# A three-layer graph network on one Trainium2 core: two bias buffers, later norm loads, and a later store of the adjacency

## The chip, the cores and the metric

The kernel runs on one core of one Trainium2 chip. The metric is the device time of one execution in microseconds (us), and lower is better. Times are given as the median of several runs. Durations of single instructions come from one profiled execution, whose own time is given below.

## The reference

Two graph networks run one after the other on 1250 nodes with 1024 features and 20000 edges. The stage that matters here is the middle of the first network, in which three layers work on a node state `h` of 256 features. Cut to what matters:

```python
h = layernorm(x, ln_in_g, ln_in_b)
h = relu(h @ W1 + b1)
h = h @ W2 + b2
for i in range(3):
    agg = segment_sum(h[src], dst, num_segments=n)
    z = h + agg                                  # (A + 1) h, A = counts of edges
    z = relu(z @ layer_Wa[i] + layer_ba[i])
    z = z @ layer_Wb[i] + layer_bb[i]            # layer_bb: the "second bias"
    z = relu(layernorm(z, layer_ng[i], layer_nb[i]))   # ng, nb: the "norm vectors"
    h = h + z
delta = relu(h @ Wd1 + bd1) @ Wd2 + bd2
return layernorm(x + delta, out_g, out_b)
```

The second network takes the mean over the neighbours with the same edges in two larger layers of 1024 features (about two thirds of the kernel's time). It uses the same adjacency matrix, without the diagonal, scaled by 1/degree.

## The kernel before

**Number format.** Every float32 operand of a matrix product is held as a high part and a low part (`split_w`, lines 133 to 135: ScalarE copies the high part at L134, VectorE takes the rest at L135), and each product is three matmuls (`mm3`, lines 122 to 125).

**Adjacency.** The 1250x1254 count matrix `A` is built in SBUF from one-hot matmuls, with the diagonal added. It serves the three layers of the first network. For the second network it is stored to memory, `A_d`, in one transfer of 6270 KB (L799), because its room in SBUF (pool tag "A") is then taken by `AD`, which holds the hidden values of the decoder (L811, written at L162 to L165 by `hidden`). It is loaded again, tile by tile, at L1165.

**One layer** (lines 769 to 808). `agg` (L667) is the product of `h` and `A` in three column chunks of 384, 512 and 358 and two halves of the features; it leaves `zh` (L672, ScalarE) and `zl` (L673, VectorE). `z1_chunk` is the product with `Wa`, bias and relu (L160 to L165). `z2_rows` takes ten row tiles: the product with `Wb`, one more matmul that adds the second bias from `bbc` (L697), the statistics, the scaling by the norm vectors `ngc` (L701) and `nbc` (L702), the sum with `h` (L704), and the split of the new `h` (L705 on ScalarE, L706 on GpSimd). The aggregation of the next layer (`agg(i + 1, ...)`) is mixed with the last rows of the present one, so that TensorE has work while rows are normalised.

**Loads of a layer.** `begin_layer(i)` (L643 to L653) loads the bias `bb[i]` as one row of 1 KB (L647), splits it with `split_w` into row 0 of `bbc` and a scratch row (L648), sends the scratch row to row 1 of `bbc` by a transfer in SBUF (L649), and loads the norm vectors, each repeated to 128 partitions (128 KB, L650 and L651). There is one `bbc`, one `ngc` and one `nbc`, so a layer's values can only be written when the last row of the layer before has been read. Layer i+1 is begun in the text behind the last rows of layer i (L793). Behind it, in the text, come for i = 0 the store of `A` (L799), the weights of layer 2 (`load_wab(2)`, L633), the decoder's bias (`load_bdo`: four loads of 256 KB at L737, then VectorE L738, L740, L743 and ScalarE L739, L742, L744) and three quarters of the decoder's second weight (`load_Wd2`, six loads at L725); for i = 1 the decoder's first weight (`load_Wd1`, L716) and the last quarter (L725).

**A ring of three.** All these raw loads, the two scratch rows of `begin_layer` among them, go through one ring of three buffers, `wraw` (L130), in the order of the text. A buffer is free again when its last reader is done.

**What sets the order.** In this stage the order on each engine is not written by hand (the hand-written parts are in `manual_schedule` blocks before and behind it). A planner lays out the program ahead of time with its own estimates of durations: on each engine it takes, among the instructions that are ready by its estimate, the one that stands first in the text. What comes out is fixed, and each engine, and SP's queue of transfers, then runs its list in that order: an instruction that has to wait holds up all that stands behind it. `tc.issue_after(x)` makes the planner place a transfer behind `x` on the same engine. All loads and stores named here are issued by SP; GpSimd issues the ones of `xo_d` (L754, L755) and `vt` (L926).

Beside the layers, `load_xo` writes x plus a bias row to memory: SP's L750 writes 5120 KB and GpSimd's L754 adds x to it in memory, 5 transfers.

Of the kernel before, what the change touches and what calls it, by code (L numbers as in the profile page):

```python
# [10 lines left out]
F32 = mybir.dt.float32  # L11
F32R = mybir.dt.float32r
# [3 lines left out]
AF = mybir.ActivationFunctionType  # L16
# [5 lines left out]
P = 128  # L22
N = 1250
NG = 4
NN = N + NG
# [3 lines left out]
DB = 256  # L29
# [26 lines left out]
def gz(t):  # L56
    return P if t < NT - 1 else N - (NT - 1) * P + NG
# [17 lines left out]
def gnn(ctx, tc, fli, general, x, es, vecs, W1, W2, b2, Wa, Wb, bb, ng, nb, Wd1, Wd2, bd2, og, ob,  # L75
        Ws0, Wn0, b0l, Ws1, Wn1, b1l, out):
    nc = tc.nc
    V, S, G, T = nc.vector, nc.scalar, nc.gpsimd, nc.tensor
# [7 lines left out]
    A_d = dram.tile([P, NT, NN], F32, name="A_d")  # L86
# [6 lines left out]
    def bcast(ap, n):  # L93
        return bass.AP(tensor=ap.tensor, offset=ap.offset, ap=[[0, P], [1, n]])
# [5 lines left out]
    ones = const.tile([P, P], F32, name="ones")  # L100
# [4 lines left out]
    def stats_to_rstd(mv, n):  # L105

        sd = small.tile([P, 1], F32, name="sd")
        S.activation(sd[:n], mv[:n, 1:2], AF.Sqrt, bias=epsc[:n])
        rs = small.tile([P, 1], F32, name="rs")
        V.reciprocal(rs[:n], sd[:n])  # L110
        return rs

    def bnstats(src, n, width):
        k = (width + 511) // 512
        st = small.tile([P, 2, 6], F32, name="st")
        for i in range(k):
            V.bn_stats(st[:n, i, :], src[:n, i * 512:min(width, i * 512 + 512)])
        mv = small.tile([P, 2], F32, name="mv")
        V.bn_aggr(mv[:n], st[:n, :k, :])
        return mv  # L120

    def mm3(ps, a_hi, a_lo, b_hi, b_lo, start, stop, go_on=False):
        T.matmul(ps, a_hi, b_hi, start=start, stop=False, skip_group_check=go_on)  # L123
        T.matmul(ps, a_hi, b_lo, start=False, stop=False, skip_group_check=go_on)  # L124
        T.matmul(ps, a_lo, b_hi, start=False, stop=stop, skip_group_check=go_on)  # L125

    def pst(name, tag="ps", dt=F32):
        return psp.tile([P, 512], dt, name=name, tag=tag)

    def wraw():  # L130
        return ring.tile([P, 512], F32, name="wraw")

    def split_w(raw, hi, lo, eng=V):
        S.activation(hi, raw, AF.Copy)  # L134
        return eng.tensor_sub(lo, raw, hi.bitcast(F32))  # L135
# [262 lines left out]
    def any_edges():  # L398

        acc = Ap.tile([P, NT, AW], F32, name="acc", tag="A")  # L400
        V.memset(acc, 0.0)
        scratch = [B1.tile([P, 8 * (PW + 2)], F32, name=f"g{s}", tag=f"h0{s}0", bufs=1) for s in "hl"] + spare
        general_adjacency(tc, psp, acc[:, :, :N], (esrc, est[:, ne:2 * ne]), ident, ones, x, A_g, xg_d, scratch)
        res = Ap.tile([P, NT, AW], F32R, name="A", tag="A")
        nc.sync.dma_start(res.bitcast(F32)[:, :, :NN], A_g)
        return res
# [6 lines left out]
    def new_h(i):  # L413
        return [[hpool.tile([P, 5, DB], F32R, name=f"h{i}{s}{j}", tag=f"h{s}{j}", bufs=2) for j in range(2)]
                for s in "hl"]
# [157 lines left out]
    for c in range(NC):  # L573
        if c == 1:
            A = any_edges() if general else Ap.tile([P, NT, AW], F32R, name="A", tag="A")
# [32 lines left out]
    B2 = tc.alloc_tile_pool(name="B2", bufs=1, side="right", reuse_waits="tile")  # L608
# [17 lines left out]
    L = {}  # L626
    loads = {}
# [8 lines left out]
        L[i] = dict(ps={}, w=(wh, wl))  # L636


    bbc = B2.tile([P, DB], F32R, name="bbc")
    S.activation(bbc[:, :P], ones, AF.Copy, scale=0.0)  # L640
    S.activation(bbc[:, P:], ones, AF.Copy, scale=0.0)

    def begin_layer(i):  # L643
        ngc, nbc = (B2.tile([P, DB], F32, name=nm_, tag=nm_, bufs=1) for nm_ in ("ngc", "nbc"))
        bbr = wraw()[0:1, :DB]
        bbl = wraw()[0:1, :DB]
        nc.sync.dma_start(bbr, bass.AP(tensor=bb.tensor, offset=bb.offset + i * DB, ap=[[DB, 1], [1, DB]]))  # L647
        split_w(bbr, bbc[0:1], bbl)  # L648
        nc.sync.dma_start(bbc[1:2].bitcast(F32), bbl)  # L649
        nc.sync.dma_start(ngc, bcast(ng[i], DB))  # L650
        loads["nb"] = nc.sync.dma_start(nbc, bcast(nb[i], DB))  # L651
        z = new_z(("zh", "zl")) + new_z(("z1h", "z1l")) if i else z_first + new_z(("z1h", "z1l"))
        L[i].update(vecs=(bbc, ngc, nbc), z=z)  # L653

    def new_z(names):
        return [[B2.tile([P, NN], F32R, name=f"{nm_}{k}", tag=f"{nm_}{k}") for k in range(2)] for nm_ in names]

    def agg(i, c, t0, t1, fs=(0, 1)):
        c0, w = CL[c]
        for f in fs:  # L660
            if t0 == 0:
                L[i]["ps"][c, f] = pst("ps_z", "pa")
            ps = L[i]["ps"][c, f]
            for t in range(t0, t1):
                n = gz(t)
                for s, hx in enumerate((hh, hl)):
                    T.matmul(ps[:, :w], hx[t // 5][:n, t % 5, f * P:(f + 1) * P], A[:n, t, c0:c0 + w],  # L667
                             start=(t == 0 and s == 0), stop=(t == NT - 1 and s == 1))
            if t1 == NT:
                zh, zl = L[i]["z"][:2]  # L670
                cs = slice(c0, c0 + w)
                S.activation(zh[f][:, cs], ps[:, :w], AF.Copy)  # L672
                V.tensor_sub(zl[f][:, cs], ps[:, :w], zh[f][:, cs].bitcast(F32))  # L673
# [14 lines left out]
    def z2_rows(i, t, nh, nl):  # L688
        n = gz(t)
        ts_ = slice(t * P, t * P + n)  # L690
        z1h, z1l = L[i]["z"][2:]
        wh, wl = L[i]["w"]
        bbc, ngc, nbc = L[i]["vecs"]
        ps = pst("ps_z2")
        for k in range(2):
            mm3(ps[:n, :DB], z1h[k][:, ts_], z1l[k][:, ts_], wh[:, 2 + k], wl[:, 2 + k], k == 0, False)
        T.matmul(ps[:n, :DB], onesr[:, :n], bbc, start=False, stop=True)  # L697
        z2 = B2.tile([P, DB], F32, name="z2", tag="z2", bufs=2)
        mv = bnstats(ps, n, DB)
        rs = stats_to_rstd(mv, n)  # L700
        V.scalar_tensor_tensor(z2[:n], ps[:n, :DB], mv[:n, 0:1], ngc[:n], ALU.subtract, ALU.mult)  # L701
        V.scalar_tensor_tensor(z2[:n], z2[:n], rs[:n], nbc[:n], ALU.mult, ALU.add)  # L702
        h = hf[t // 5][:n, t % 5]
        V.scalar_tensor_tensor(h, z2[:n], 0.0, h, ALU.max, ALU.add)  # L704
        S.activation(nh[t // 5][:n, t % 5], h, AF.Copy)  # L705
        G.tensor_sub(nl[t // 5][:n, t % 5], h, nh[t // 5][:n, t % 5].bitcast(F32))  # L706
# [39 lines left out]
    def load_xo():  # L746

        o = C3.tile([P, D], F32, name="o", tag="wt")
        nc.sync.dma_start(o, bcast(ob, D))
        nc.sync.dma_start(xo_d.rearrange("t p f -> p t f"), o.unsqueeze(1).broadcast_to([P, NT, D]))  # L750
        rows = xo_d.rearrange("t p f -> (t p) f")
        for t in range(0, NT, 2):
            r0, r1 = t * P, min(N, t * P + 2 * P)
            G.dma_start(rows[r0:r1], x[r0:r1], accum_op=ALU.add, max_dma_last_dim=8 * D)  # L754
        G.dma_start(rows[N:NN], xg_d, accum_op=ALU.add, max_dma_last_dim=4 * D)  # L755

    z_first = new_z(("zh", "zl"))
    load_wab(1)
    load_wab(0)
    begin_layer(0)  # L760
    load_xo()
    for t in range(EARLY + 1, NT):
        for half, cs in zip(sums, HALVES):
# [5 lines left out]
    for i in range(3):  # L769
        nh, nl = new_h(i)  # L770

        def rows(*ts):
            for t in ts:
                z2_rows(i, t, nh, nl)

        z1_chunk(i, 0)
        z1_chunk(i, 1)
        rows(0, 1)
        agg(i, 2, 0, 5, (0,))
        rows(2, 3)  # L780
        agg(i, 2, 5, NT, (0,))
        if i == 1:
            degrees()
        rows(4)
        agg(i, 2, 0, NT, (1,))
        rows(5, 6)
        if i == 2:
            break
        z1_chunk(i, 2)
        hh, hl = nh, nl  # L790
        agg(i + 1, 0, 0, 4)
        rows(7, 8, 9)
        begin_layer(i + 1)  # L793
        agg(i + 1, 1, 0, 4)
        agg(i + 1, 0, 4, 7)
        agg(i + 1, 1, 4, 7)
        if i == 0:
            with tc.issue_after(loads["nb"].ins):
                nc.sync.dma_start(A_d, A.bitcast(F32)[:, :, :NN])  # L799
            load_wab(2)  # L800
            load_bdo()
            for k in range(3):
                load_Wd2(k)
        else:
            load_Wd1()
            load_Wd2(3)
        agg(i + 1, 0, 7, NT)
        agg(i + 1, 1, 7, NT)


    AD = Ap.tile([P, NT, AW], F32R, name="AD", tag="A")  # L811
# [349 lines left out]
    A, loaded = {}, []  # L1161
# [523 lines left out]
```

## Time and profile before

| | us |
|---|---|
| median of 3 runs (lowest, highest) | 915.53 (914.59, 917.31) |
| time of the profiled execution | 917.94 |
| its span, first to last instruction | 916.1 |
| TensorE busy in the span | 891.3 (97%) |
| VectorE busy | 649.6 (71%) |
| ScalarE busy | 393.0 (43%) |
| GpSimd busy | 79.2 (9%) |
| mean granted clock of TensorE | 0.990 |

The profiled execution took 1.84 us more than its span and 2.41 us more than the median of the runs. TensorE is busy for nearly the whole span, so a change can only win where TensorE waits, and it loses wherever it makes TensorE wait. The three layers lie from 121 to 248 us. Busy time of TensorE is a union of overlapping matmuls: one of 256 columns is shown with 0.28 us, but the next one starts 0.12 us later. Where a matter of a few us is at stake, the starts of the matmuls say more than the busy share.

### The profile page before, as it was taken

Reading aid. Unit: us, or ns where it says so; the run is one execution under the profiler, and the core shown is the slowest. Engines: PE = TensorE matmul, PEld = TensorE weight load, DVE = VectorE, ACT = ScalarE, POOL = GpSimd, SP = SyncE. Lnnn points to the kernel's source line nnn. Section 1 sums busy time; section 2 is a strip of 40 time slices with the busy share of each in tenths; the row PEclk is TensorE's granted clock in tenths of the full one; section 3 lists DMA queues with packets and bytes.
Section 4 is the critical chain, followed back from the end, with each engine's and each line's share of the span. In section 5 each row is a group of like instructions: output and inputs, shape, how many; then the busy total and the mean of one; then the engine's idle time right before and its main releaser. Section 6 shows DMA issues by size and latency. Waiting matters only on the chain.

```text
span 916.1 us, 13254 instructions
## 1 busy us (share of the span) xinstructions
PE 891.3 (97%) x4783; PEld 783.0 (85%) x4783; DVE 649.6 (71%) x1335; ACT 393.0 (43%) x760; POOL 79.2 (9%) x106
## 2 busy tenths in 40 slices
PE   7899999999999999999999999999999999999995
PEld 5799999888987778999988888889999888888884
DVE  7999778597976776565586775447566776776883
ACT  3776524455467872111234355443112233333552
POOL 2223345121301000000000000000000000000000
PEclk8999999999999999999999999999999999999998
DMA  8310069953207569896622246538885722222223
GB/s 255 106 42 2 1 254 204 335 151 104 70 24 253 185 241 333 311 301 230 222 72 81 81 141 204 180 121 304 289 276 197 230 70 81 78 80 74 69 95 133
DMA packets 83668, 148.40 MB, mean 162 GB/s; under 512 B 8296, under 2 KB 31995, under 8 KB 83082
## 3 DMA queue, kind: packets, MB, share of 16 engines
q1 hardware_dynamic: 77206, 126.92, 41.4%
q0 software_dynamic: 2176, 10.27, 4.4%
q10 hardware_dynamic: 4212, 10.27, 3.0%
q8 instruction: 39, 0.64, 0.3%
q14 instruction: 35, 0.29, 0.1%
HBM read 103.37 MB, written 49.21 MB: 167 GB/s over the span
## 4 chain that ended last, share of the span: by engine, by line
PE 84%; DVE 8%; issue 3%; ACT 2%; DMA 1%; POOL 0%; POOLq 0%; ACTq 0%; DVEq 0%
PE ps_A L1237 20%; PE ps_m L123 14%; PE ps_m L125 14%; PE ps_m L124 14%; PE ps_z L667 4%; PE ps_dd L123 2%; PE ps_dd L125 2%; PE ps_dd L124 2%; PE pa L367 1%; PE ps_y L123 1%; PE pt L989 1%; PE pt L1258 1%; PE ps_y L124 1%; PE ps_y L125 1%; PE ps_z L124 1%
## 5 line engine op out<-in xcount | busy, mean ns | idle before, releaser
L123 PE MATMUL ps_m<-w,th 128*128 128x512 f32 x520 | 204.0, 392 | 0.0
L125 PE MATMUL ps_m<-w,th 128*128 128x512 f32 x520 | 202.5, 389 | 0.0
L124 PE MATMUL ps_m<-w,th 128*128 128x512 f32 x520 | 202.3, 389 | 0.0
L1237 PE MATMUL ps_A<-A,qh 128*128 128x418 f32 (+1 forms) x480 | 170.8, 356 | 0.0
L1237 PE MATMUL ps_A<-A,ql 128*128 128x418 f32 (+1 forms) x480 | 169.3, 353 | 0.0
L125 PEld LDWEIGHTS ps_m<-w,th 128*128 128x128 f32 x520 | 97.6, 188 | 20.6
L124 PEld LDWEIGHTS ps_m<-w,th 128*128 128x128 f32 x520 | 97.7, 188 | 19.9
L123 PEld LDWEIGHTS ps_m<-w,th 128*128 128x128 f32 x520 | 97.7, 188 | 19.6
L135 DVE TENSOR_TENSOR w<-stage,w 128x512 fp32r<-128x512 f32 x65 | 44.7, 690 | 68.1 <-ACT w L134 67.7
L1237 PEld LDWEIGHTS ps_A<-A,qh 128*128 128x128 f32 (+1 forms) x480 | 90.3, 188 | 2.0 <-DVE c L1220 0.4
L1237 PEld LDWEIGHTS ps_A<-A,ql 128*128 128x128 f32 (+1 forms) x480 | 90.7, 189 | 1.4
L134 ACT ACTIVATE w<-stage 128x512 fp32r<-128x512 f32 x65 | 40.7, 629 | 118.9 <-PE ps_m L125 78.9
L1242 DVE TENSOR_TENSOR MT<-ps_A,dgb 128x418 f32<-128x418 f32 x48 | 25.5, 586 | 64.4 <-PE ps_A L1237 64.4
L1198 ACT ACTIVATE qh<-qraw 128x1280 fp32r<-128x1280 f32 (+3 forms) x28 | 21.5, 808 | 104.3 <-PE ps_A L1237 87.0
L123 PE MATMUL ps_y<-h0h,w1h 128*128 128x256 f32 (+2 forms) x160 | 53.3, 333 | 0.4 <-ACT h0h L455 0.4
L135 DVE TENSOR_TENSOR w<-wraw,w 128x512 fp32r<-128x512 f32 x39 | 26.9, 689 | 32.7 <-ACT w L134 32.6
L1326 DVE TENSOR_TENSOR c<-ps_m,c 128x512 f32<-128x512 f32 (+1 forms) x65 | 40.9, 682 | 8.8 <-PE ps_m L125 8.7
L124 PE MATMUL ps_y<-h0l,w1h 128*128 128x256 f32 (+2 forms) x160 | 45.8, 286 | 1.0 <-DVE h0l L457 0.9
L125 PE MATMUL ps_y<-h0h,w1l 128*128 128x256 f32 (+2 forms) x160 | 45.5, 284 | 0.0
L1067 ACT ACTIVATE th<-XT 128x640 fp32r<-128x640 f32 x48 | 34.2, 725 | 20.5 <-DVE MT L1242 20.5
L134 ACT ACTIVATE w<-wraw 128x512 fp32r<-128x512 f32 x39 | 24.5, 628 | 41.9 <-PE ps_m L125 21.3
L1068 DVE TENSOR_TENSOR th<-XT,th 128x640 fp32r<-128x640 f32 x48 | 39.5, 822 | 0.0
(311 smaller groups left out, 1829.7 us busy)
## 6 DMA issues: line engine op xcount, KB each, us to landing
A<-A_d SPq DMA_DIRECT2D x20, 627.0 KB
w_d<-stage SPq DMA_DIRECT2D x43, 256.0 KB
stage<-w_d SPq DMA_DIRECT2D x43, 256.0 KB
stage<-in_l_W_neigh_dram SPq DMA_DIRECT2D x42, 256.0 KB
stage<-in_l_W_self_dram SPq DMA_DIRECT2D x28, 256.0 KB
A_d<-A SPq DMA_DIRECT2D x1, 6270.0 KB
wraw<-in_l_W_neigh_dram SPq DMA_DIRECT2D x22, 256.0 KB
w_d<-wraw SPq DMA_DIRECT2D x21, 256.0 KB
```

Of the source, the lines that this page charges most:

```text
L123: T.matmul(ps, a_hi, b_hi, start=start, stop=False, skip_group_check=go_on)
L124: T.matmul(ps, a_hi, b_lo, start=False, stop=False, skip_group_check=go_on)
L125: T.matmul(ps, a_lo, b_hi, start=False, stop=stop, skip_group_check=go_on)
L134: S.activation(hi, raw, AF.Copy)
L135: return eng.tensor_sub(lo, raw, hi.bitcast(F32))
L667: T.matmul(ps[:, :w], hx[t // 5][:n, t % 5, f * P:(f + 1) * P], A[:n, t, c0:c0 + w], start=(t == 0 and s == 0), stop=(t == NT - 1 and s == 1))
L1067: S.activation(hi, src, AF.Copy)
L1068: V.tensor_sub(lo, src, hi.bitcast(F32))
L1198: S.activation(q[0][:, t0:t1], raw[:, t0:t1], AF.Copy)
L1237: T.matmul(pss[j][c][:, :w], qs[j][s][:n, t], A_of(t)[:n, c0:c0 + w], start=start and s == 0, stop=stop and s == 1)
L1242: V.tensor_mul(MT[:, f, c0:c0 + w], pss[j][c][:, :w], dgb[:, c0:c0 + w])
L1326: V.tensor_add(c, ps[:n], c if last or M in (6, 7) else c11[:n, t])
```

## The change

The bias buffer `bbc` is made twice, and layer i uses number i mod 2. The two loads of the norm vectors move out of `begin_layer` into a function `load_norm`, which is called at the end of the loop's body, behind the other loads; for layer 0 it is called directly behind `begin_layer(0)`. The store of `A` moves from the loop's pass i = 0, where it stood behind layer 1's norm loads and ahead of `load_wab(2)`, to pass i = 1, behind layer 2's norm loads.

```diff
-    bbc = B2.tile([P, DB], F32R, name="bbc")
-    S.activation(bbc[:, :P], ones, AF.Copy, scale=0.0)
-    S.activation(bbc[:, P:], ones, AF.Copy, scale=0.0)
+    bbcs = [B2.tile([P, DB], F32R, name=f"bbc{i}") for i in range(2)]
+    for bbc in bbcs:
+        S.activation(bbc[:, :P], ones, AF.Copy, scale=0.0)
+        S.activation(bbc[:, P:], ones, AF.Copy, scale=0.0)
 
     def begin_layer(i):
-        ngc, nbc = (B2.tile([P, DB], F32, name=nm_, tag=nm_, bufs=1) for nm_ in ("ngc", "nbc"))
+        bbc = bbcs[i % 2]
         bbr = wraw()[0:1, :DB]
         bbl = wraw()[0:1, :DB]
         nc.sync.dma_start(bbr, bass.AP(tensor=bb.tensor, offset=bb.offset + i * DB, ap=[[DB, 1], [1, DB]]))
         split_w(bbr, bbc[0:1], bbl)
         nc.sync.dma_start(bbc[1:2].bitcast(F32), bbl)
+        z = new_z(("zh", "zl")) + new_z(("z1h", "z1l")) if i else z_first + new_z(("z1h", "z1l"))
+        L[i].update(bbc=bbc, z=z)
+
+    def load_norm(i):
+        ngc, nbc = L[i]["norm"] = [B2.tile([P, DB], F32, name=nm_, tag=nm_, bufs=1) for nm_ in ("ngc", "nbc")]
         nc.sync.dma_start(ngc, bcast(ng[i], DB))
         loads["nb"] = nc.sync.dma_start(nbc, bcast(nb[i], DB))
-        z = new_z(("zh", "zl")) + new_z(("z1h", "z1l")) if i else z_first + new_z(("z1h", "z1l"))
-        L[i].update(vecs=(bbc, ngc, nbc), z=z)
...
-        bbc, ngc, nbc = L[i]["vecs"]
+        bbc, (ngc, nbc) = L[i]["bbc"], L[i]["norm"]
...
     begin_layer(0)
+    load_norm(0)
     load_xo()
...
         if i == 0:
-            with tc.issue_after(loads["nb"].ins):
-                nc.sync.dma_start(A_d, A.bitcast(F32)[:, :, :NN])
             load_wab(2)
             load_bdo()
             for k in range(3):
...
             load_Wd2(3)
         agg(i + 1, 0, 7, NT)
         agg(i + 1, 1, 7, NT)
+        load_norm(i + 1)
+        if i == 1:
+            with tc.issue_after(loads["nb"].ins):
+                nc.sync.dma_start(A_d, A.bitcast(F32)[:, :, :NN])
```

## The prediction, made before the changed kernel was run

> **What bounds the kernel now.** I began with the busy shares and the chain of work that ended last: TensorE, busy 97% and 84% of the chain. So a gain must come from places where TensorE stands, and the next view is who it waited for during the layers (176 to 222 us, layer 1's pass). The columns are the total wait, the times, and the longest.
>
> ```profile
> PE ps_z L124 <- DVE zl L673: 1.2, 1, 1.2
> PE ps_z L125 <- DVE z1l L165: 0.8, 1, 0.8
> PE ps_z L123 <- ACT z1h L162: 0.4, 1, 0.4
> PE ps_z L667 <- POOL h1l L706: 0.2, 1, 0.2
> ```
>
> The same view for layer 0's pass (138 to 176 us) is empty. Overlapping matmuls hide part of the loss, so I measure it by starts. The first 512-column z1 matmul starts at 139.53 in layer 0, 177.54 in layer 1 and 222.31 in layer 2. Layer 0 takes 38.01 us, layer 1 44.77 us, with the same matmuls and the six of the degrees (L619), which displace 2.1 us (186.95 to about 189.06). **Layer 1 loses 44.77 - 38.01 - 2.1 = 4.66 us.** That is what there is to win. Four places, each measured against the usual distance of starts, make 4.3 of it: 1.9 in the last z1 chunk (its twelve matmuls span 3.68 us, 1.80 in layer 0), 0.55 before 202.97, 0.9 before 208.44, 0.9 in the aggregation at 215 to 217.4.
>
> Why do they occur? The timeline of SP's queue (start, duration, line):
>
> ```profile
> 128.81 0.64 SPq L649 DMA_DIRECT2D bbc<-wraw  x1
> 129.55 1.18 SPq L647 DMA_DIRECT2D wraw<-in_layer_bb_dram  x1
> 139.36 0.38 SPq L633 DMA_DIRECT2D wraw<-in_layer_Wa_dram  x1
> 164.09 0.54 SPq L649 DMA_DIRECT2D bbc<-wraw  x1
> 164.72 0.54 SPq L633 DMA_DIRECT2D wraw<-in_layer_Wb_dram  x1
> ...
> 166.43 0.64 SPq L799 DMA_DIRECT2D A_d<-A  x1
> 168.95 2.22 SPq L737 DMA_DIRECT2D wraw<-in_bd_dram  x1
> 171.28 1.68 SPq L737 DMA_DIRECT2D wraw<-in_out_b_dram  x1
> 173.51 0.92 SPq L737 DMA_DIRECT2D wraw<-in_bd_dram  x1
> 192.22 0.33 SPq L737 DMA_DIRECT2D wraw<-in_out_b_dram  x1
> ```
>
> and its waits:
>
> ```profile
> SPq L649 <- DVE wraw L135: 27.9, 3, 24.3
> SPq L737 <- DMA wraw<-in_out_b_dram: 16.5, 1, 16.5
> SPq L633 <- DMA bbc<-wraw: 8.6, 1, 8.6
> ```
>
> Layer 1's bias sits in the ring from 129.55 and stops SP for 24.3 us, since its split has to wait for layer 0's last row (162.1). Then the store of 6270 KB goes out ahead of the decoder's bias loads, and the first of ob's lands only at 173.51 + 0.92 + 16.5 = 190.9. So the fourteen pieces of work on bdo and the six splits of Wd2 fall on 191 to 211, among layer 1's rows:
>
> ```profile
> 195.51 0.69 DVE L738 TENSOR_TENSOR wraw<-wraw 128x512 f32<-128x512 f32 x1 [1.31 <-DMA wraw<-in_out_b_dram]
> 196.23 0.69 DVE L743 TENSOR_TENSOR wraw<-wraw,bdo 64x512 f32<-64x512 f32 x1
> 196.95 0.16 DVE L110 RECIPROCAL rs<-sd 128x1 f32<-128x1 f32 x1
> 197.03 0.51 DVE L673 TENSOR_TENSOR zl<-ps_z,zh 128x358 fp32r<-128x358 f32 x1
> ```
>
> TensorE's longest wait (1.2 us) is for that zl, which stands in line behind a subtraction that waits for ob. The wait at 202.97 is ScalarE's L742, L134 and L744 ahead of z1h, the one at 208.44 VectorE's Wd2 splits ahead of z1l, and the one at 216 is row 9: its bias matmul comes 22.3 us after the layer's mark in layer 0 and 31.6 in layer 1.
>
> **The change, part by part.**
>
> Second `bbc`: two more fills on ScalarE, 2 x 0.29 us at about 120.9. The list behind them waits 2.62 us for a load at 125.86, and the split of tile 9 at 121.78 is needed by matmuls at 134.5, so they cost nothing; without that cover 0.6.
>
> Layer 1's bias no longer waits for row 9. Its two ring buffers come free about 20 us earlier; Wb of layer 2 and the first bd load take them. Wa and Wb themselves still wait for layer 0's last row (one tile with the weights of layer 0), so the next buffers come free at the splits, 167.3 in the trace.
>
> The store leaves the queue there: the loads behind it get the engines. A load of 256 KB without it took 2.7 us at 201.55 (landed by 204.23). Work to place: on VectorE 6 x 0.69 for bdo and 6 x 0.69 for Wd2, 8.3 us; on ScalarE 8 x 0.63 and 6 x 0.63, 8.8 us. Room between 160 and 180: VectorE is idle for 9.0 us there (busy 4.42, 1.98, 1.93 and 2.65 in the four windows of 5 us), ScalarE for 11.7. From 180 to 190 VectorE is busy 9.4 of 10. Since the loads come three at a time from about 165, the bias part and some splits fit ahead of the rows and a few splits don't. I take back 0.5 us for those (lowest 0, highest the whole 4.3).
>
> The norm loads move behind others. They are freed by row 9 (L702 ends at 165.7) and needed at 183.2; if a ring load stands ahead of them they wait a few us of these 17. In layer 2 they are freed at 214.3 and needed at 229.0. Nothing; once 17 us are used up, each us costs one.
>
> Layer 2: Wd2's last quarter (VectorE L135 at 223.89, ahead of z1l) comes before the boundary. TensorE loses 0.25 us at 225.97 to it; gain 0.25.
>
> The store in its new place: freed by nbc of layer 2, so at 214.3 + 0.9 less what layer 1 has gained by then (3.4), about 211.8. Its own time is bounded by 17.0 us (6.42 MB at the 377 GB/s mean of 170 to 185 us) and 24.5 us (166.43 to 190.9). It lands between 229 and 236. DMA there is 0.0 to 0.56 busy. The new waiter is `AD`, which takes A's room: its first write is ScalarE's L162 at 244.44, 240.4 after the gain. Margin 4 to 11 us: nothing. Behind it on SP stand weights used at 284 and `ogc`, issued at 248. GpSimd's `vt` loads run on another queue and are needed from 252.6.
>
> Sum: 4.3 + 0.25 - 0.5 = **4.0 us less**. The profiled execution, 917.94, would become 913.9; it stands 2.41 above the median, so from 915.53 I forecast **911.5**. TensorE waits for nothing over 0.2 us from 330 on, so the gain should last to the end.
>
> **A rule against the row.** Layer 0's bias row of 1 KB, issued at 128.81 behind the 5120 KB store of L750, lands when SP's wait ends, 139.36: 10.5 us. Layer 1's bias load stands right behind it. Its split could now be listed early, ahead of ScalarE's first zh (135.04). The Trainium skill, DMA: Bandwidth & Descriptors, section Latency and other measured facts, puts the fixed cost of a transfer at some 2 us; by that, an estimate, the row would be there at 132 and this would cost nothing. The measured 10.5 us decides.
>
> **Rivals.**
>
> *Half a gain.* Either the planner puts the bias split ahead of zh: zh slips to 139.4 + 0.4, its first pair ends at about 140.3 and z1, which starts at 137.43, loses 2.9 (3.9 with zl behind it): 4.0 - 3.4, 914.9. Or the bdo and Wd2 work lands on the busy 181 to 200 and gives back half: 913.5. For it: instructions standing ready first in the text go first. Against it: the planner put L738 behind four rows of layer 1, close to when ob landed, so it does know of big transfers. Middle 914.2.
>
> *Slower: the decoder waits for the store.* If the weight loads of L1036 (220.97 to 224.94 now, each waiting for a ring buffer) are listed ahead of the norm loads, the store goes out at 225 and lands at 242 to 249.5, and AD's first write, with ScalarE's list behind it and soon all four banks of TensorE, waits up to 9.1 us. It decides from an issue at 215.9 (slow store) or 223.4 (fast). Price at the slow end 9.1 - 4.0: up to 920.6; I name 919. Against it: the norm loads come first in the text and are ready before most ring buffers.
>
> *More.* All 4.66 goes, and the work moved off VectorE also frees the wait for hT at 241.54 (0.76) and the two of 0.4 behind it: 909.3.
>
> **Chances.** Forecast (910 to 913) 0.56, half a gain 0.22, slower 0.14, more 0.08. A measurement can tell about 0.3%, 2.75 us, from no change. Faster by over that (under 912.8): 0.53 + 0.08 = 0.61. Within it: 0.03 + 0.21 = 0.24. Slower: 0.01 + 0.14 = 0.15. Range: 908.5 to 917.0, which leaves out most of the slower case and the edge of the best.
>
> **What would show it.** Right: layer 1 from mark to mark at about 40.5 us, no 24.3 us wait of L649, the first ob load landed by about 172, TensorE's waits for zl, z1h and z1l gone, the store issued at about 212 and no wait of AD's writers for it. Wrong: ScalarE or VectorE waiting for the bias row at 131 to 140; L701 waiting for ngc; L162 waiting for the store; Wd2 splits still ahead of z1l at 203 to 208.

## The result, and the profile after

The changed kernel takes 918.97 us (median of 14 runs, 916.66 to 920.51), the kernel before, run beside it, 917.24 (14 runs, 914.59 to 919.38). The ratio of the runs is **1.0027, 95% interval 1.0017 to 1.0037: about 2.5 us slower** (the two medians are 1.7 us apart). The forecast was 911.5, the range ended at 917.0, and the sign was wrong. The profiled execution took 919.0 us with a span of 917.2 (before: 917.94 and 916.1).

I measure it as the prediction did, from the start of the first 512-column z1 matmul of one layer to that of the next, and from layer 2's to the decoder's first matmul (`ps_dd`). The marks lie at 138.33, 179.97, 224.57 and 249.20 us, before at 139.53, 177.54, 222.31 and 247.83:

| us | before | after | difference |
|---|---|---|---|
| layer 0 (to layer 1's mark) | 38.01 | 41.64 | +3.63 |
| layer 1 (to layer 2's mark) | 44.77 | 44.60 | -0.17 |
| layer 2 (to the decoder) | 25.52 | 24.63 | -0.89 |
| sum | 108.30 | 110.87 | +2.57 |

The sum agrees with the ratio. (The two profiled executions differ by 1.1 us only, mainly because the one of before reaches its first mark 1.20 us later.) Layer 1, from which 4 us were to come, gave almost nothing, and layer 0, which had no loss at all, lost 3.6. Here is who TensorE waits for from 174 to 222 us (total, times, longest), to be read beside the four lines of before at the head of the prediction:

```profile
PE ps_z L123 <- ACT zh L676: 2.0, 2, 1.8
PE ps_d L619 <- DVE z L705: 1.5, 2, 1.2
PE ps_z L124 <- DVE zl L677: 1.1, 3, 0.4
PE ps_z L125 <- DVE z1l L165: 0.2, 1, 0.2
```

The waits have moved. TensorE now stands at the head of layer 1 for zh and zl, the evacuations of the aggregation, and then at the degrees (L619), whose PSUM bank is freed late by a row's L705. The timeline of SP's queue shows the change doing what it says:

```profile
144.54 0.54 SPq L650 DMA_DIRECT2D bbc<-wraw  x1
145.17 0.54 SPq L633 DMA_DIRECT2D wraw<-in_layer_Wb_dram  x1
150.22 0.35 SPq L741 DMA_DIRECT2D wraw<-in_bd_dram  x1
163.97 0.35 SPq L741 DMA_DIRECT2D wraw<-in_out_b_dram  x1
165.26 0.33 SPq L656 DMA_DIRECT2D ngc<-in_layer_ng_dram  x1
...
171.81 0.33 SPq L741 DMA_DIRECT2D wraw<-in_out_b_dram  x1
175.94 9.21 SPq L729 DMA_DIRECT2D wraw<-in_Wd_dram  x6
```

Layer 1's bias is through at 144.54 instead of 164.09, and no store stands ahead of the decoder's bias loads. `bdo`, the decoder's bias, holds bd2 - ob in three bf16 parts. Each half of 512 columns needs one load of bd2 and one of ob, and then a chain of seven pieces of work in turn, three subtractions on VectorE and four copies on ScalarE. The first load of ob, which needs the third buffer of the ring, waits until 163.97, when the split of Wa gives that buffer back. On VectorE (first line) and ScalarE (the others) the work that waits for it then looks like this:

```profile
171.08 0.69 DVE L742 TENSOR_TENSOR wraw<-wraw 128x512 f32<-128x512 f32 x1 [4.18 <-DMA wraw<-in_out_b_dram]
```

```profile
171.81 0.63 ACT L743 ACTIVATE bdo<-wraw 128x512 bf16<-128x512 f32 x1 [4.46 <-DVE wraw L742]
173.20 1.27 ACT L746 ACTIVATE bdo<-wraw 32x512 bf16<-32x512 f32 x2 [0.76 <-DVE wraw L744]
175.22 0.63 ACT L748 ACTIVATE bdo<-wraw 64x512 bf16<-64x512 f32 x1 [0.76 <-DVE wraw L747]
175.95 0.63 ACT L743 ACTIVATE bdo<-wraw 128x512 bf16<-128x512 f32 x1
176.48 0.85 ACT L676 ACTIVATE zh<-ps_z 128x384 fp32r<-128x384 f32 x2
```

Both engines stand over 4 us for ob, 7.1 us under way (163.97 to 171.08). Then the chain of the first half goes to and fro between them, each step waiting for the other engine, and takes 4.8 us for 2.1 us of work on VectorE and 2.5 on ScalarE. Layer 1's first zh stands behind it in ScalarE's list and comes at 176.48. In the kernel before, it waited for its matmul alone, and the chain stood behind layer 1's row 3:

```profile
171.79 0.49 ACT L672 ACTIVATE zh<-ps_z 128x384 fp32r<-128x384 f32 x1 [0.71 <-PE ps_z L667]
```

### The profile page after: what moved, and what is told of

It reads as the page before. It is cut to its first block, busy times and chain, and to the rows that moved or that the text cites. A ratio compares the mean times of both kernels' runs of the same rounds, so it can differ in the third digit from the quotient of the medians.

```text
span 917.2 us, 13254 instructions
## 1 busy us (share of the span) xinstructions
PE 892.2 (97%) x4783; PEld 783.2 (85%) x4783; DVE 649.2 (71%) x1335; ACT 393.1 (43%) x762; POOL 77.8 (8%) x106
## 4 chain that ended last, share of the span: by engine, by line
PE 83%; DVE 9%; issue 3%; ACT 2%; DMA 2%; POOL 0%; POOLq 0%; SPq 0%; DVEq 0%; ACTq 0%
PE ps_A L1244 20%; PE ps_m L123 14%; PE ps_m L125 14%; PE ps_m L124 14%; PE ps_z L671 4%; PE ps_dd L123 2%; PE ps_dd L125 2%; PE ps_dd L124 2%; DVE hf L708 1%; PE pa L367 1%; PE ps_y L123 1%; PE pt L996 1%; PE pt L1265 1%; DVE z L706 1%; PE ps_y L124 1%
```

## The theories, and experiments on which part it is

**Theory A**: the loss is this chain, listed ahead of layer 1's zh and zl and waiting there for ob. **Theory B**: it is the store in its new place, by its traffic after 215 us. **Theory C**: it is the norm vectors' new place. Four kernels do parts of the change.

### Two bias buffers alone

```diff
-    bbc = B2.tile([P, DB], F32R, name="bbc")
+    bbcs = [B2.tile([P, DB], F32R, name=f"bbc{i}") for i in range(2)]
...
+        bbc = bbcs[i % 2]
```

> The kernel before with the two bias buffers alone: norm vectors and store stay where they were. Theory A (the loss is the chain that makes bdo: it is now listed on ScalarE and VectorE ahead of layer 1's own zh and zl, and stands there for ob's load, 7 us under way): in this kernel's order the first half of the chain stands ahead of zh of 128x384 and the second half with the Wd2 splits behind row 3, as before, so layer 0 (first 512-column z1 matmul of layer 0 to that of layer 1) should be 40 to 42 us against 38.0 before and 41.6 in the changed kernel, layer 1 about 44.8, and the time 2 to 4 us above before. Theory B (the store's new place costs it, by its traffic after 215 us): the store hasn't moved, so the time is that of before, within 1 us. Theory C (the norm loads' new place): the same as B.

Measured: 919.97 us, ratio to before 1.0040 (1.0023 to 1.0056); layer 0 41.32 us, layer 1 46.90, layer 2 24.64. Layer 0 and the time are those of theory A. Layer 1 lost 2.1 us more than I had expected: the second half of the chain runs at 195 to 201 us there, among the rows, as it did before, while the first half has already cost its time in layer 0.

### The store one layer later alone

```diff
-            with tc.issue_after(loads["nb"].ins):
-                nc.sync.dma_start(A_d, A.bitcast(F32)[:, :, :NN])
...
         agg(i + 1, 1, 7, NT)
+        if i == 1:
+            with tc.issue_after(loads["nb"].ins):
+                nc.sync.dma_start(A_d, A.bitcast(F32)[:, :, :NN])
```

> The kernel before with the store alone one layer later; one bias buffer, norm loads as before. Theory A: without the store ahead of them the loads of bd2 and ob land at about 174 us instead of 190, and the order puts the chain of bdo among the four zh and zl of layer 1, so layer 0 is 40 to 43 us and the time 1 to 4 us above before. Theory B: slower by the whole 2.5 us, but with layer 0 at 38.0 and the loss behind 215 us. Theory C: as before, within 1 us.

Measured: 918.59 us, ratio 1.0022 (1.0010 to 1.0034); layer 0 41.47, layer 1 42.75, layer 2 26.47. The loss is in layer 0, where the store is not, so theory B falls. (Layer 2, where the store now runs, is 0.95 us longer here, but 0.89 shorter in the changed kernel.) With one buffer only, this kernel makes the same loss: freeing the queue is enough to pull the chain forward.

### The changed kernel with the store put back

```diff
-        if i == 1:
+        if i == 0:
             with tc.issue_after(loads["nb"].ins):
```

> The changed kernel with the store put back into the pass of layer 0, behind the norm vectors of layer 1. Theory A: the first half of bdo's chain is still listed ahead of zh, its ob is issued ahead of the store and lands at about 171 us, so layer 0 is 40 to 42 us; the second half and Wd2 stand behind row 3 again and layer 1 is about 44.8; the time is 2 to 4 us above before, so no better than the changed kernel. Theory B: the time goes back to that of before, or below it by what the early bias brings (0 to 4 us faster than the changed kernel). Theory C: no nearer to before than the changed kernel, with layer 0 unlike theory A at 38 to 39.

Measured: 920.04 us, ratio 1.0039 (1.0024 to 1.0055); layer 0 43.37, layer 1 43.69, layer 2 24.64. No nearer to before than the changed kernel, as theory A has it. Layer 0 was longer than expected, layer 1 shorter.

### The norm vectors later alone

```diff
         agg(i + 1, 1, 7, NT)
+        load_norm(i + 1)
+        if i == 0:
+            with tc.issue_after(loads["nb"].ins):
+                nc.sync.dma_start(A_d, A.bitcast(F32)[:, :, :NN])
```

> The kernel before with the loads of the norm vectors alone put behind the layer's other loads (the store behind them, as they are what it waits for). Theory A: the order keeps bdo's chain behind row 3, so layer 0 stays at 38.0, layer 1 at about 44.8, and the time within 1 us of before. Theory B: within 1 us of before. Theory C: 1.5 to 3 us slower than before.

Measured: 916.98 us, ratio 1.0004 (0.9994 to 1.0014); 38.01, 44.75, 25.62. No effect, and here the chain stands behind row 3. Theory C falls. (The store waits for the norm vectors and so moves in the text with them; it went out at 168.21, behind one load of bd2 and ahead of both loads of ob.) In all four kernels the time goes with the place of the chain.

## Is it the wait or the work?

**Theory A1**: what costs is that the chain stands ahead of zh and waits there for a late load. **Theory A2**: what costs is its work and that of the Wd2 splits, on two engines that have no room for it anywhere near.

### The chain held behind zl

```diff
-            V.tensor_sub(d, d, o)
-            S.activation(bdo[:, fs], d, AF.Copy)
+            with tc.issue_after(loads["zl"].ins):
+                V.tensor_sub(d, d, o)
+                S.activation(bdo[:, fs], d, AF.Copy)
...
         load_norm(i + 1)
+        if i == 0:
+            load_bdo()
+            for k in range(3):
+                load_Wd2(k)
```

(`loads["zl"]` is the last L677 of the aggregation; the calls stood ahead of its last tiles.)

> The changed kernel with bdo and Wd2(0..2) written behind layer 1's whole aggregation, and the first two steps of each half of bdo's chain held on ScalarE and VectorE until the last zl of that aggregation is issued; the loads are issued in the same order as in the changed kernel. Theory A1 (what costs is that the chain stands, waiting for ob, ahead of zh and zl): layer 0 goes back from 41.6 to 38.0 to 39 us, layer 1 stays at 44.6 to 46, and the time is 1.5 to 4 us below the changed kernel. Theory A2 (what costs is the chain's and the splits' work itself on two engines that have no room at the head of a layer, wherever it stands): layer 0 38 to 39, but layer 1 grows by as much, 47 to 48, and the time is that of the changed kernel within 1 us.

Measured: 915.11 us, ratio to before 0.9986 (0.9975 to 0.9997), against 1.0027 for the changed kernel: 3.8 us below it. Layer 0 38.84, layer 1 43.34, layer 2 24.51. Same loads, same work, another place in two lists: 2.8 us of layer 0 are back and layer 1 didn't grow. This is theory A1. VectorE's first step of the chain comes behind the last zl and waits for nothing, and the first zh comes at 171.16:

```profile
176.24 0.68 DVE L743 TENSOR_TENSOR wraw<-wraw 128x512 f32<-128x512 f32 x1
```

### Three kernels that I expected to be faster

```diff
-        for i in range(2):
...
+        V.memset(bdo, 0.0)
```

> The changed kernel without bdo's four loads and its chain (bdo is set to zero, so the decoder's biases are left out). It prices the chain as a whole. Theory A1: layer 0 38 to 38.5, and layer 1 at most 44.6 with the Wd2 splits; the time 3.5 to 6 us below the changed kernel. Theory A2: the same or more, 5 to 8 below, since the work that is gone is worth its length. A loss that has nothing to do with the chain would leave layer 0 above 40.

```diff
             load_wab(2)
-            load_bdo()
...
             load_Wd2(3)
+            load_bdo()
```

> The changed kernel with bdo built in the pass of layer 1, behind Wd1 and Wd2(3), so at the head of layer 2; Wd2(0..2) stay in the pass of layer 0 and are listed now in layer 0's tail. Theory A1: bdo's loads have landed by the time its chain is reached, so it waits for nothing: layer 0 38 to 39, layer 1 43 to 45, layer 2 (to the first decoder matmul) 24.6 to 26.5, and the time 2 to 5 us below the changed kernel, so 0 to 3 below before. Theory A2: the loss comes back in layer 2 (27 to 28.5), the time within 1.5 us of the changed kernel.

```diff
-            d, o = wraw(), wraw()
-            for to, row in ((d, bd2), (o, ob)):
-                nc.sync.dma_start(to, bcast(row[fs], 512))
-            V.tensor_sub(d, d, o)
+            d = wraw()
+            nc.sync.dma_start(d, bcast(bd2[fs], 512))
+            V.tensor_sub(d, d, xo_o[0][:, fs])
```

> The changed kernel with bdo reading ob from the copy that load_xo holds on the chip already, so that its chain waits for bd2 alone and two loads of 256 KB and two buffers of the ring are saved; bdo's first half is now listed in layer 0's tail, the second half and Wd2(0) still ahead of zh. Theory A1: the stand of 4.2 to 4.5 us for ob is gone; layer 0 38 to 40, and the time 1.5 to 4.5 us below the changed kernel. Theory A2: the same work stands at the same place, layer 0 40.5 to 42 and the time within 1 us of the changed kernel.

Measured: without bdo 925.57 us, ratio 1.0105 (1.0088 to 1.0121), layer 0 54.03; bdo in layer 2's pass 930.06, 1.0155 (1.0131 to 1.0179), layer 0 52.64; ob kept 927.74, 1.0125 (1.0106 to 1.0143), layer 0 53.92. All three missed by 10 us or more, and the traces say why. In the kernel without bdo, the room in the ring lets the first Wd2 load go out at 148.01, and its split is now listed in layer 0's tail, ahead of rows and of a zh of the third chunk. These are the waits of ScalarE (140 to 184 us) and TensorE (138 to 184):

```profile
ACT wd L134 <- DMA wraw<-in_Wd_dram: 20.1, 4, 16.6
```

```profile
PE ps_z L123 <- ACT zh L676: 13.4, 1, 13.4
```

In the kernel with bdo in layer 2's pass ScalarE stands 16.0 us for the same load. In the kernel with ob kept it is bd2 that VectorE waits for:

```profile
DVE wraw L743 <- DMA wraw<-in_bd_dram: 14.0, 1, 14.0
```

The order on each engine is written before the kernel runs, and here it counts on an early issue being an early landing. In the kernel without bdo the Wd2 load of 256 KB landed at 163.7, 15.7 us after its issue: the 16 DMA engines are full until about 168 us, and the next experiment shows with what: the five transfers in which GpSimd's queue adds x to a copy of ob in memory. The three kernels make the changed kernel's mistake one place earlier, and at a higher price.

### The same order without the traffic

```diff
-        for t in range(0, NT, 2):
-            r0, r1 = t * P, min(N, t * P + 2 * P)
-            G.dma_start(rows[r0:r1], x[r0:r1], accum_op=ALU.add, max_dma_last_dim=8 * D)
-        G.dma_start(rows[N:NN], xg_d, accum_op=ALU.add, max_dma_last_dim=4 * D)
```

> The changed kernel without the five transfers in which GpSimd's queue adds x to ob's copy in memory (x is left out of the sum that the decoder adds to), which keep the 16 DMA engines full from about 130 to 168 us in the changed kernel; the order on ScalarE and VectorE is the same, with bdo's first half ahead of layer 1's zh. It tells the landing from the place. Theory A1 (the chain is late because its loads land late): ob, still issued at about 164 us behind the split that frees its buffer, lands within 3 us of it instead of 7, the chain starts at 167 to 168 instead of 171.8, ahead of the time at which zh is wanted (171.8 in before), and layer 0 is 38 to 39.5 us instead of 41.6. Theory A2 (the place and the work alone): layer 0 stays at 40.5 to 42. The time as a whole can fall by more than layer 0 does, since the traffic is gone elsewhere too; the verdict is on layer 0.

Measured: 915.71 us, ratio 0.9982 (0.9972 to 0.9992); layer 0 38.82, layer 1 44.89, layer 2 24.62. Here are 160 to 165 us in the changed kernel and then in this one (busy time of PE, PEld, DVE, ACT and POOL, granted clock, DMA share, GB/s):

```profile
160.00:165.00 5.00, 5.00 (x30) 4.38 (x29) 4.83 (x16) 2.23 (x6) 1.22 (x2) 1.00 1.00 210
160.00:165.00 5.00, 5.00 (x29) 4.30 (x28) 4.93 (x17) 2.24 (x6) 1.15 (x1) 1.00 0.04 14
```

The DMA share falls from 1.00 to 0.04. ScalarE at the head of layer 1:

```profile
167.88 0.63 ACT L743 ACTIVATE bdo<-wraw 128x512 bf16<-128x512 f32 x1 [0.78 <-DVE wraw L742]
169.27 1.27 ACT L746 ACTIVATE bdo<-wraw 32x512 bf16<-32x512 f32 x2 [0.76 <-DVE wraw L744]
...
173.35 0.85 ACT L676 ACTIVATE zh<-ps_z 128x384 fp32r<-128x384 f32 x2
```

The chain is at the same place in the list, but ob, issued at 163.71, is there by 167.16, 3.5 us later, and the first zh comes 3.1 us sooner. TensorE waits 0.2 us for it instead of 2.0. **So 41.64 - 38.82 = 2.8 us of layer 0's loss are the late landing.** Layer 1 stays at 44.89, with the chain and the Wd2 splits in the same order at the head of the layer, late load or not.

### Without bdo, the Wd2 splits held behind zh

```diff
-            split_w(raw, hi[:, fs], lo[:, fs], V)
+            with tc.issue_after(loads["zh"].ins):
+                split_w(raw, hi[:, fs], lo[:, fs], V)
```

(On top of the kernel without bdo, with `load_Wd2` called behind the aggregation; `loads["zh"]` is its last L676.)

> The changed kernel without bdo's loads and chain (bdo is zero: the decoder's biases are left out), and with the Wd2(0..2) splits held on ScalarE until layer 1's last zh is issued, so that they can't be listed in layer 0's tail as in the run without bdo before it, where the first split stood 16.6 us for its load. Theory A1: nothing stands ahead of zh, layer 0 is 38.0 to 38.5 us, layer 1 41 to 43.5, and the time is 4 to 7 us below the changed kernel. If layer 0 stays above 40, the chain was not the cause.

Measured: 912.81 us, ratio 0.9953 (0.9939 to 0.9967), 6.8 us below the changed kernel; layer 0 38.84, layer 1 41.65, layer 2 24.65. The two slow kernels above with neither the chain nor these splits in layer 1 took 40.40 (without bdo) and 40.39 us (bdo in layer 2's pass) for that layer, so the splits, held behind zh, cost 1.25 us in it. The kernel with the chain behind zl has 43.34, so the chain's work, placed well, costs about 1.7 us more: a part of theory A2 holds. Layer 0 was expected at 38.0 to 38.5; 0.8 us stay that the chain doesn't explain.

### bdo in layer 2's pass, held behind zl

```diff
         load_norm(i + 1)
+        if i == 0:
+            for k in range(3):
+                load_Wd2(k)
         if i == 1:
+            load_bdo()
```

(With both holds of above.)

> The changed kernel with the Wd2(0..2) splits held behind layer 1's last zh, and bdo loaded and built in the pass of layer 1, its chain held behind layer 2's last zl of the first two chunks, so among the evacuations of layer 2's z1. Theory A1: layer 0 38.0 to 38.5, layer 1 41 to 43.5 as in the kernel without bdo, layer 2 24.6 to 26.5 since the chain's loads land behind the norm vectors and ahead of the store; the time 3 to 6 us below the changed kernel, 0.5 to 3.5 below before. Theory A2: layer 2 grows to 27 or more and the time is within 1.5 us of before.

Measured: 915.59 us, ratio 0.9984 (0.9975 to 0.9994); 38.85, 41.67, 28.67. Layers 0 and 1 are those of A1, layer 2 that of A2, and the time fits both. SP's queue, and VectorE's second half of the chain:

```profile
210.12 0.64 SPq L818 DMA_DIRECT2D A_d<-A  x1
218.78 0.33 SPq L742 DMA_DIRECT2D wraw<-in_out_b_dram  x1
```

```profile
235.92 0.69 DVE L744 TENSOR_TENSOR wraw<-wraw 128x512 f32<-128x512 f32 x1 [1.50 <-DMA wraw<-in_out_b_dram]
```

The second ob waits for a ring buffer, goes out behind the store and lands 17.1 us later, with layer 2's last zl listed behind it (TensorE waits 2.0 us for that zl). The same trap, a third time.

### ob kept, so that both loads go ahead of the store

The edit is that of "ob kept" above, on the kernel just shown.

> The kernel with bdo held in layer 2's pass, and ob read from the copy that load_xo keeps on the chip, so that both loads of bd2 are issued ahead of the store. Theory A1 (that kernel's layer 2 took 28.7 us instead of 24.6 because the second half of the chain stood for a load of ob that went out 8.7 us behind the store): layer 2 falls to 24.6 to 26, layer 0 and layer 1 stay at 38.8 and 41.7, and the time is 2 to 4 us below that kernel, 3 to 5 us below before. Theory A2 (the chain's work itself costs 4 us wherever it stands): layer 2 stays at 28 or more.

Measured: 914.62 us, ratio 0.9971 (0.9959 to 0.9983); 38.82, 41.67, 26.15. Layer 2 falls by 2.5 us, so most of the 4 us was the load; the 26.15 - 24.65 = 1.5 us that stay are near the 1.7 of the chain's work in layer 1. The time fell by 1.2 us only, against 2 to 4 expected; the intervals of the two ratios overlap, so no more can be read from it.

### The bias split put back where it was

```diff
-        split_w(bbr, bbc[0:1], bbl)
+        with tc.issue_after(loads["nh"].ins) if i == 1 else nullcontext():
+            split_w(bbr, bbc[0:1], bbl)
```

> The same kernel with the split of layer 1's bias held on ScalarE until the last normalized row of layer 0 is copied, where the kernel before has it for want of a second buffer. It prices the part of the change that was meant to help, in the layer that it touches. If the early split is what makes layer 0 38.8 us instead of 38.0 with nothing ahead of zh, layer 0 goes back to 38.0 and the time falls by up to 0.8 us (no more than the runs can tell); the rest of the loads, held behind zh anyway, lose nothing. If layer 0 stays at 38.8, the 0.8 us come from elsewhere in the new order; if it grows, the early split was worth something.

Measured: 913.89 us, ratio 0.9958 (0.9942 to 0.9973); 38.02, 41.69, 26.14. Layer 0 is back to 38.0 exactly: the early split, and the order that comes with it, cost 0.8 us, and since the loads behind it are held anyway, nothing is lost without it. This is the fastest complete kernel of the study: about 3.9 us below before, 6.3 below the changed kernel. Since its second bias buffer is no longer used early, none of this gain comes from that buffer, the heart of the change.

## Why the prediction was wrong, point by point

- **The account of layer 1's loss (4.66 us) was right.** With neither the chain nor the splits in it, layer 1 takes 40.40 instead of 44.77: 4.4 of the 4.66 are gone. That is no gain for the kernel as long as this work costs more elsewhere.
- **The step that failed**: "Since the loads come three at a time from about 165, the bias part and some splits fit ahead of the rows". Two things in it. First, a load was costed at the 2.7 us of one at 201.55, when DMA was idle; at 164 it took 7.1, because GpSimd's transfers filled the engines. (With the store issued behind it, it took 7.7 and 8.4 us, in the kernel with two bias buffers alone and in the one with the store put back.) The prediction looked for what the store had delayed and didn't look at what else was under way. The Trainium skill, DMA: Bandwidth & Descriptors, section Issuing engines are not separate DMA queues, says that transfers started by different engines share the same 16; the runs agree: the same ob load took 7.1 us beside GpSimd's transfers and 3.5 without them.
- Second, **idle time was added up as room**. VectorE was idle for 9 us between 160 and 180, but the load that starts the work came at 171, the work is a hand-over of 4.8 us per half, and engines that run in order put it ahead of zh, whose turn came at 171.8. The bounds (0 to 4.3 us taken back) knew no end at which work moved forward costs more than the gain. In the sum 4.3 + 0.25 - 0.5 it is the last term that was mis-sized, what the work costs at its new place: where it has 0.5, layer 0 lost 2.8 us, and layer 1 kept 4.2 (44.60 against 40.40). With the 0.8 us of the bias split, the sum by measured sizes is 4.37 + 0.89 - 4.20 - 2.82 - 0.80 = -2.56, the loss of the table.
- The planner "does know of big transfers" was half right. By the lists it reckons with the store on SP's queue: where ob's load stands behind the store (the second half in the kernels with two bias buffers alone and with the store put back) the chain is listed behind row 3. It doesn't reckon with GpSimd's transfers: without them the order at the head of layer 1 is the same, and the three kernels with a stand of 14 to 17 us listed a load's user some 15 us before its landing.
- **Layer 1's bias no longer waits: right.** It was split at 141.9 without a wait, so the first half of the rival "half a gain" didn't happen. Its price, put at nothing, was 0.8 us. Nothing that waited for it tells whether the row was there after 2 or after 10.5 us: it was first used 13.6 us after its issue (128.36). The rival's second half, bdo and Wd2 on busy engines, pointed to the right work, but to the rows and not to the aggregation's end.
- **The norm loads: right**, nothing (ratio 1.0004 alone).
- **The store in its new place: right.** It went out at 215.74 (forecast 211.8), DMA was busy 0.94 and 1.02 of 215 to 225 and 225 to 235 us and 0.22 of the next ten, and `AD`'s first write at 245.47 waits for no transfer. The rival that ended slower didn't happen; the kernel is slower by a mechanism that no rival had. Layer 2 gained 0.89 instead of 0.25.
- **The base**: the three runs shown had a median of 915.53, later ones 916.2 to 917.5. This shifted the forecast by some 1.7 us; it doesn't change the sign.

The 3.63 us of layer 0 are shown by single changes: 2.8 (the landing) and 0.8 (the bias split). The two prices come from two different kernels; that they add up to 3.6 speaks for them. For layer 1, the runs show that 4.2 us hang on the chain and on the Wd2 splits; how they divide in the changed kernel I haven't separated.

## What to carry to other kernels

When a wait goes, work moves forward, and in a kernel whose order is laid out in advance it may move ahead of something that the bounding engine needs: ask what each freed load's user will stand in front of, and when that load lands with everything that is on the DMA engines at that time. Idle time of an engine is room only from the moment at which the work's input is there, and for as long as its hand-overs take. A hold that puts such work behind the evacuations was worth 3.8 us here, nearly what the forecast had hoped for from the whole change.

## What the runs showed of the hardware that I had not expected

A load of 256 KB took 2.7 us with DMA idle, 3.5 without the added x, 7.1 and 15.7 beside GpSimd's transfers, and 17.1 behind the store of 6270 KB: a factor of six by what else is under way.

A long stand costs more than its length. The kernel without bdo in stretches of 5 us, with the same columns as above:

```profile
150.00:155.00 5.00, 2.16 (x18) 1.86 (x16) 0.00 (x0) 0.00 (x0) 0.00 (x0) 1.00 1.02 218
155.00:160.00 5.00, 0.00 (x0) 0.00 (x0) 0.00 (x0) 0.00 (x0) 0.00 (x0) 0.68 1.03 225
160.00:165.00 5.00, 0.00 (x0) 0.00 (x0) 0.61 (x1) 1.27 (x4) 0.26 (x1) 0.50 1.00 215
165.00:170.00 5.00, 4.44 (x14) 4.16 (x15) 5.00 (x17) 3.17 (x10) 2.65 (x4) 0.50 0.52 166
170.00:175.00 5.00, 5.00 (x35) 4.97 (x34) 3.71 (x12) 1.08 (x4) 3.10 (x2) 0.96 0.14 52
```

TensorE's last matmul ends at 152.2. The clock is halved from about 156.8 (0.68 of 5 us is 1.8 us at full and 3.2 at half speed) and is full again at about 170.4, 4.8 us after work resumes at 165.56. So some 2.4 us are lost on top of the 13.4. The changed kernel's waits of up to 1.8 us leave the clock at 1.00. The Trainium skill, TensorE: Matmul & The Clock Gate, Part 1, puts each of the two changes after at least one window of about 3.4 us, in windows that run freely; the 4.6 and 4.8 us read here, between one window and two, agree.
